# A graph layer with linear attention: mixed queries two chunks ahead, and VectorE reading PSUM in place of a second SBUF tensor

## The chip, the cores and the metric

The kernel runs on one core of a Trainium2 chip. The metric is the device time of one execution in microseconds (us). The engines are named as the profile names them: PE is TensorE's matmul pipe and PEld its weight load, DVE is VectorE, ACT is ScalarE, POOL is GpSimd, SP is SyncE, which here only issues DMAs. "Kernel before" and "changed kernel" are the two versions.

## The reference

N = 10000 nodes with D = 512 features, 160000 edges sorted by target node, everything in f32. One layer computes

```python
xn = layernorm(x)
# node sums (a graph convolution)
gnn = relu(segment_sum((xn @ W)[src] * edge_weight[:, None], dst) + bias)
# linear attention, 8 heads of 64
q, k, v = split(xn @ w_qkv.T)
q = softmax(q, over the 64 features of a head) * 64 ** -0.5
k = softmax(k, over the nodes)
mix = layernorm_gamma((q @ (k.T @ v)) @ w_out.T)          # context per head
x1 = x + gnn + mix
# experts: the mean over all nodes of layernorm(x1) chooses them, for all nodes alike
t = layernorm(x1)
p = softmax(mean(t, over nodes) @ router_w.T); two best -> weight of each of 6 experts
out = x1 + sum_e weight_e * (gelu(t @ W1[e] + b1[e]) @ W2[e] + b2[e])
```

## The kernel before, in words

**Chunks.** The nodes go in 20 chunks: 19 of 512 rows and one of 272. A chunk is a tile of 128 partitions (68 in the last) by 4 row blocks (`SUB`, index `s`) by 512 features.

**Stages**, with the places in the profiled execution's span where they lie:

1. 0 to about 195 us: rows of x are normalised (`normal_rows`) and written to `xn_d` in DRAM; the first three chunks of the next stage are already done here, and the tables of the edges are made.
2. to about 1285 us: for each chunk, keys `pk` and queries `pq` (L203 in `times`), exp of both on ACT, the softmax of the queries on DVE (`softmax_rows`, L182 to L188: a reduce over each head, a reciprocal, a multiply), the transposed queries `qT` written to DRAM, and the product `pc` (L780) of keys and normalised rows, summed into `G`.
3. to about 1355 us: `G`, the values' and the output's weights are folded into one 512 x 512 matrix `mix` (products `pctx`, `pmix`).
4. to about 2290 us, the attention stage: for each chunk, `attention` (L890 to L911) and the node sums (L929 to L946).
5. to the end, the feed-forward part (L1096 and around), which both versions have alike, but for the mean.

**Edges.** The 160000 edges are 1250 tiles of 128. `edges_in` gathers the source rows of each tile from `xn_d` by an indirect DMA that POOL issues (L483, tile `msg`, 24 buffers, up to 16 tiles ahead) and builds a selection matrix `sel` (six buffers) on DVE: for a whole group of 8 or 4 tiles at once, one comparison of a row of numbers with each edge's place in its window (L489), one multiplication by the edge's weight (L492), and a copy of one column (L495). `edges_summed` multiplies `sel` and `msg` on PE (`pm`, L504), ACT copies the result to `part` and stores it in `part_d` (L507, L508). There are 201 such groups. They are laid between the other matmuls of stages 2 and 4: after every product the code calls `work`, which adds the product's estimated PE time to a clock and then does as many groups as that time divided by `PACE` allows. So a smaller `PACE` puts more edge tiles into stage 2.

**Attention stage.** `attention(c)` loads the transposed queries `qT` (one buffer) and the rows of x again as `xt` (two buffers), multiplies by `mix` (`po`, L203), copies to `ot` on ACT (L903; three buffers), takes the row statistics (`row_stats`, bn_stats at L160, square root on ACT at L168), and on DVE normalises with gamma (L907) and adds `xt` (L909). It takes a function `beside`, which it calls ahead of its last row block. For the node sums of chunk c, `at` holds the rows gathered from `part_d` (`gathered`, L865, two buffers, an indirect DMA by POOL for each row block, after `far_enough` has put in the edge groups that those rows need). `nodes_rows` transposes `at` into `aT` (one buffer; PE's transposes `pt`, ACT's copies L197) and starts the gather of chunk c + 1. Then come four products with the graph weights (`pg`), the bias (L933, from PSUM into `et`, which is `at` itself), and one instruction over all four row blocks that takes the larger of `et` and 0 and adds `ot` (L934). The sum is stored as `x1_d` (L935), its row statistics are taken, it is normalised once more (L178) into `at`, or in the last chunk into the buffer `wg`, and the normalised rows are added up in `xsum` (L946) for the mean that chooses the experts.

In the kernel before, `attention(0)` precedes the loop, and iteration c calls `attention(c + 1)` with `nodes_rows` of chunk c as `beside`. So PE's order in an iteration is: three row blocks of `po` for chunk c + 1, the transposes for chunk c, the fourth `po`, four products `pg` for chunk c; edge groups stand between them.

**What sets the order.** PE's instructions run in the order in which the code lists them (`manual_schedule`). The other engines' orders are made by the planner of the tile framework from its own estimate of costs. SP's DMAs (`qT`, `xt`, the stores of `x1_d`) are one queue, ACT's (`qT_d`, `part_d`) another; POOL issues all gathers in one order.

**PSUM.** A pool of six banks serves `pk`, `pq`, `pc`, `po`, `pg` and the transposes in turn; two more serve `pm`. A bank is taken again when the engine that reads it is done.

**Mean.** After stage 4, `mean_row` sums `xsum` over partitions with a matmul against ones, adds the last chunk's normalised rows in the same way, and DVE multiplies by 1/N.

Of the kernel before, what the change touches and what calls it, by code (L numbers as in the profile page):

```python
# [9 lines left out]
F32 = mybir.dt.float32  # L10
I32 = mybir.dt.int32
AF = mybir.ActivationFunctionType
ALU = mybir.AluOpType
AX = mybir.AxisListType
# [3 lines left out]
P = 128  # L18
SQ = 32
SUB = 4  # L20
EPS = 1e-5
HEAD = 64
# [3 lines left out]
WIN = P // GROUP  # L26
# [1 line left out]
EARLY = 3  # L28
ROWS_SOON = 5
PRODUCT = 0.83  # L30
PACE = 0.93

AT_HAND = [(5, 320), (7, 384), (9, 448), (11, 512), (13, 576), (14, 640), (15, 672), (16, 704), (17, 736), (18, 756)]
CARRIES = [0, 128, 224, 320, 384, 448, 512, 576, 640, 672, 704, 736, 756]
# [12 lines left out]
def gps_layer_kernel(  # L47
# [19 lines left out]
    nc = tc.nc  # L67
    N, D = x.shape
# [18 lines left out]
    NCH = len(chunks)  # L87
# [5 lines left out]
    const = ctx.enter_context(tc.tile_pool(name="const", bufs=1))  # L93
# [34 lines left out]
    gamma_b = const.tile([P, D], F32, name="gamma_b")  # L128
    nc.scalar.dma_start(gamma_b, gamma.to_broadcast([P, D]))
    row_of = const.tile([P, NCH, SUB], I32, name="row_of")  # L130
    stats2 = const.tile([P, NCH, SUB, 2], F32, name="stats2")


# [42 lines left out]
    def normalize(o, t, r, mv, pool=0):  # L176
        for s in range(SUB):
            (nc.vector if s < SUB - pool else nc.gpsimd).tensor_scalar(  # L178
                o[:r, s, :], t[:r, s, :], mv[:r, s, 0:1], mv[:r, s, 1:2],
                op0=ALU.subtract, op1=ALU.mult)  # L180

    def softmax_rows(q, r, s):  # L182

        q3 = q[:r, s, :].rearrange("p (h e) -> p h e", e=HEAD)
        qs = small.tile([P, D // HEAD], F32, name="qs")
        nc.vector.tensor_reduce(qs[:r], q3, axis=AX.X, op=ALU.add)
        nc.vector.reciprocal(qs[:r], qs[:r])
        nc.vector.tensor_tensor(q3, q3, qs[:r, :, None].to_broadcast([r, D // HEAD, HEAD]), ALU.mult)  # L188

    def transposed(o, t, r, psum, tag, by_act=(1, 3)):  # L190

# [141 lines left out]
    with ExitStack() as ph:  # L333
# [139 lines left out]
        def edges_in(i):  # L473

            t0, batch = tiles_of(i)
            n = min(GROUP * batch, NET - t0)
            m = [None] * n
            for j in range(batch):
                for h in range(GROUP):
                    k = h * batch + j  # L480
                    if k < n:
                        m[k] = pools["m"].tile([P, D], F32, name="msg")
                        nc.gpsimd.indirect_dma_start(  # L483
                            out=m[k], out_offset=None, in_=xn_d,
                            in_offset=bass.IndirectOffsetOnAxis(ap=src_sb[:, t0 + k : t0 + k + 1], axis=0))
            sel = ew.tile([P, 2 * GROUP, WIN], F32, name="sel", bufs=6)
            if n < GROUP * batch:
                nc.vector.memset(sel[:, n:, :], 0.0)
            nc.vector.tensor_tensor(  # L489
                sel[:, :n, 1:], iota_w[:, None, :].to_broadcast([P, n, WIN - 1]),  # L490
                place[:, t0 : t0 + n, None].to_broadcast([P, n, WIN - 1]), ALU.is_equal)
            nc.vector.tensor_tensor(  # L492
                sel[:, :n, 1:], sel[:, :n, 1:],
                w_sb[:, t0 : t0 + n, None].to_broadcast([P, n, WIN - 1]), ALU.mult)
            nc.vector.tensor_copy(sel[:, :n, 0:1], on_w[:, t0 : t0 + n, None])  # L495
            return batch, m, sel

# [17 lines left out]
        held = {"edges": []}  # L515
# [229 lines left out]
        for c, (_, r) in enumerate(chunks):  # L745
# [23 lines left out]
            for s in range(SUB):  # L769
                pq = psum.tile([P, D], F32, name="pq", tag="ps")  # L770
                times(pq, xnT, s, r, wq)
                work(KB * PRODUCT)
                nc.scalar.activation(qt[:r, s, :], pq[:r], AF.Exp, scale=usable[:r])
                softmax_rows(qt, r, s)
            if c + 1 < NCH:
                xnT = turned_rows(c + 1, xn_next)
            for cb in range(KB):
# [63 lines left out]
        wg = wq  # L841
        nc.sync.dma_start(wg, gnn_w.rearrange("(k p) d -> p k d", p=P))
        nc.vector.memset(xsum, 0.0)
        io = query_ctx.enter_context(tc.tile_pool(name="c_io", bufs=2, side="right", reuse_waits="tile"))

        def far_enough(c):
# [28 lines left out]
            return qT  # L875

        def rows_again(c):
            xt = io.tile([P, SUB, D], F32, name="xt")
            nc.sync.dma_start(xt[: chunks[c][1]], tokens(x, c))
            return xt  # L880

# [6 lines left out]
        def attention(c, beside):  # L888


            r = chunks[c][1]
            qT = queries_in(c)
            xt = rows_again(c)
            ot = io.tile([P, SUB, D], F32, name="ot", bufs=3)
            for s in range(SUB):
                if s == SUB - 1:
                    beside()
                po = psum.tile([P, D], F32, name="po", tag="ps")
                times(po, qT, s, r, mix)
                put_out(KB * PRODUCT)  # L900
                if c == s == 0:
                    held["at"] = gathered(0)
                nc.scalar.copy(ot[:r, s, :], po[:r, :])  # L903
            mv = small.tile([P, SUB, 2], F32, name="mv")
            row_stats(ot, r, mv)
            for s in range(SUB):
                nc.vector.scalar_tensor_tensor(ot[:r, s, :], ot[:r, s, :], mv[:r, s, 0:1],  # L907
                                               gamma_b[:r], op0=ALU.subtract, op1=ALU.mult)
                nc.vector.scalar_tensor_tensor(ot[:r, s, :], ot[:r, s, :], mv[:r, s, 1:2],  # L909
                                               xt[:r, s, :], op0=ALU.mult, op1=ALU.add)  # L910
            return ot  # L911

        ot_next = attention(0, lambda: None)
        for c, (_, r) in enumerate(chunks):
            ot, at = ot_next, held["at"]
            aT = io.tile([P, KB, SUB * P], F32, name="aT", bufs=1)

            def nodes_rows():
# [1 line left out]
                if c + 1 < NCH:  # L920
                    held["at"] = gathered(c + 1)

            if c + 1 < NCH:
                ot_next = attention(c + 1, nodes_rows)
            else:
                nodes_rows()

            et = at
            for s in range(SUB):  # L929
                po = psum.tile([P, D], F32, name="pg", tag="ps")  # L930
                times(po, aT, s, r, wg)
                put_out(KB * PRODUCT)
                nc.vector.tensor_tensor(et[:r, s, :], po[:r, :], bias_b[:r], ALU.add)  # L933
            nc.vector.scalar_tensor_tensor(ot[:r], et[:r], 0.0, ot[:r], op0=ALU.max, op1=ALU.add)  # L934
            nc.sync.dma_start(x1_d[c], ot[:r])  # L935
            mv = stats2[:, c]
            row_stats(ot, r, mv)

            nt = et if c < NCH - 1 else wg
            normalize(nt, ot, r, mv)  # L940

            nc.vector.scalar_tensor_tensor(mv[:r, :, 0], mv[:r, :, 0], -1.0, mv[:r, :, 1],
                                           op0=ALU.mult, op1=ALU.mult)
            if c < NCH - 1:
                for s in range(SUB):
                    nc.vector.tensor_tensor(xsum[:r], xsum[:r], et[:r, s, :], ALU.add)  # L946
            if c == NCH - 3:
                sums_of_weights()
            if c == NCH - 2:
# [54 lines left out]
    def mean_row():  # L1004
        r = chunks[-1][1]
        nc.tensor.matmul(pmean, ones, xsum, start=True, stop=False)
        for s in range(SUB):
            nc.tensor.matmul(pmean, ones[:r], last[:r, s, :], start=False, stop=s == SUB - 1)
        mean_ctx.close()
        nc.vector.tensor_scalar(mean, pmean, 1.0 / N, None, op0=ALU.mult)  # L1010

    def mean_column():
        pr = psum_r.tile([P, D], F32, name="pr")
# [300 lines left out]
```

## Time and profile before

| | us |
|---|---|
| median of 10 executions | 3664.21 (3653.14 to 3674.59) |
| profiled execution | 3669.89 |
| its span | 3667.9, mean granted PE clock 0.958 |
| PE busy | 3370.1 (92%) |
| DVE busy | 1701.9 (46%) |
| POOL busy | 1470.4 (40%) |
| ACT busy | 794.9 (22%) |
| gathers of edges, L483 on POOL | 1250, 1257.0 in all, 1.006 each |
| `sel`, L489 and L492 on DVE | 201 each, 71.2 and 71.2 in all |
| L934 on DVE | 19 of 128 x 2048, 2.293 each |
| L178 on DVE in the attention stage | 76 of 128 x 512, 0.562 each |

The profile is of one execution. Busy times count an engine's own instructions, not its waits or its issuing of DMAs. The view in slices cuts the span into 40 equal parts and gives busy shares in tenths. In a list of waits, a line names the waiting engine, its tile and line, then what ended the wait. "issue" there means that the profile shows nothing that was waited for, "remote" that a signal came from another engine without its instruction being matched. In a line of the timeline the brackets hold the idle time of that engine just before the instruction. Idle time of an engine that is not the bound costs nothing by itself.

### The profile page before, as it was taken

To read this page: it belongs to the slowest core of one execution; us is meant where nothing else is said; L and a number is where in the kernel's file an instruction comes from. 1 tells how busy PE (TensorE), PEld (TensorE's weight loads), DVE (VectorE), ACT (ScalarE), POOL (GpSimd) and SP (SyncE) were. 2 spreads that over 40 slices of the span, in tenths; PEclk is the share of its full clock that TensorE was granted. 3 is DMA by queue.
4 is the path that set the end of the run, shared out by engine and by line. 5 is a ranking of instruction groups with operands and counts; after the bars stand their busy time and mean duration, and the time that the engine had idled before them with its cause. 6 is when DMAs were issued, how large, how long until landed. Compare 5 with 4: busy or idle time off the path is not lost. (4 is left out here: it accounts for less than half of the span.)

```text
span 3667.9 us, 36451 instructions
## 1 busy us (share of the span) xinstructions
PE 3370.1 (92%) x12967; PEld 1950.5 (53%) x12967; DVE 1701.9 (46%) x3899; ACT 794.9 (22%) x1626; POOL 1470.4 (40%) x1472
## 2 busy tenths in 40 slices
PE   6999998989999858988888999899999999999998
PEld 3433333333343323333333334788888888888877
DVE  7723333333343324545555557554454454454542
ACT  4411111111111111111121121322222222222221
POOL 7666666656666665767767652000000000000000
PEclk9999999999999978989999999999999999999999
DMA  9677777767777777878888875122212212221210
GB/s 360 253 230 213 246 224 230 235 207 233 229 225 224 212 237 235 269 255 297 285 277 290 277 253 150 45 76 58 69 58 58 81 47 58 81 55 49 81 36 36
DMA packets 218326, 644.91 MB, mean 176 GB/s; under 512 B 35486, under 2 KB 75422, under 8 KB 193786
## 3 DMA queue, kind: packets, MB, share of 16 engines
q0 software_dynamic: 108208, 354.02, 31.5%
q1 hardware_dynamic: 67656, 168.51, 14.4%
q10 hardware_dynamic: 42266, 119.91, 8.5%
q8 instruction: 106, 1.74, 0.2%
q14 instruction: 90, 0.74, 0.1%
HBM read 485.32 MB, written 157.00 MB: 175 GB/s over the span
## 5 line engine op out<-in xcount | busy, mean ns | idle before, releaser
L483 POOL DMA_INDIRECT msg<-xn_d,src_sb x1250 | 1257.0, 1006 | 661.6 <-issue 291.3
L504 PE MATMUL pm<-msg,sel 128*32 128x512 f32 x2504 | 380.1, 618 | 63.8 <-issue 51.0
L203 PE MATMUL pg<-wq,aT 128*128 128x512 f32 (+1 forms) x640 | 310.5, 633 | 41.6 <-issue 30.0
L780 PE MATMUL pc<-xn,ek 128*128 128x512 f32 (+1 forms) x640 | 307.4, 624 | 38.7 <-issue 22.1
L203 PE MATMUL po<-G,qT 128*128 128x512 f32 (+1 forms) x640 | 308.0, 626 | 18.1 <-issue 17.9
L203 PE MATMUL pq<-wq,xnT 128*128 128x512 f32 (+1 forms) x640 | 289.9, 601 | 7.5 <-issue 6.7
L203 PE MATMUL pk<-wk,xnT 128*128 128x512 f32 (+1 forms) x640 | 285.7, 597 | 0.6 <-issue 0.5
L507 ACT COPY part<-pm 128x512 f32<-128x512 f32 x201 | 117.8, 586 | 762.3 <-remote 365.0
L504 PEld LDWEIGHTS pm<-msg,sel 128*32 128x32 f32 x2504 | 72.6, 110 | 337.4 <-issue 304.4
L203 PEld LDWEIGHTS pg<-wq,aT 128*128 128x128 f32 (+1 forms) x640 | 120.7, 197 | 232.6 <-issue 200.9
L780 PEld LDWEIGHTS pc<-xn,ek 128*128 128x128 f32 (+1 forms) x640 | 122.8, 200 | 192.7 <-issue 168.1
L203 PEld LDWEIGHTS po<-G,qT 128*128 128x128 f32 (+1 forms) x640 | 121.0, 197 | 194.5 <-issue 184.4
L489 DVE TENSOR_TENSOR sel<-iota_w,place 128x248 f32<-128x248 f32 (+2 forms) x201 | 71.2, 354 | 325.1 <-remote 193.0
L1096 PE MATMUL px<-xnT,w_sb 128*128 128x256 f32 (+1 forms) x800 | 204.8, 379 | 11.1 <-DVE u L1131 11.0
L203 PEld LDWEIGHTS pq<-wq,xnT 128*128 128x128 f32 (+1 forms) x640 | 117.9, 188 | 178.4 <-issue 172.5
L203 PEld LDWEIGHTS pk<-wk,xnT 128*128 128x128 f32 (+1 forms) x640 | 117.7, 188 | 164.7 <-issue 158.4
L1096 PE MATMUL px<-w_sb,hh 128*128 128x256 f32 (+1 forms) x800 | 186.2, 380 | 0.0
L1096 PE MATMUL py<-xs,w_sum 128*128 128x256 f32 (+1 forms) x800 | 185.0, 374 | 0.0
L1096 PE MATMUL py<-w_sum,hh 128*128 128x256 f32 (+1 forms) x800 | 179.2, 379 | 0.0
L1096 PEld LDWEIGHTS px<-xnT,w_sb 128*128 128x128 f32 x800 | 150.7, 192 | 34.3 <-DVE u L1131 14.5
L160 DVE BATCH_NORM_STATS2 st<-ot 128x6 f32<-128x512 f32 (+1 forms) x160 | 106.7, 677 | 125.9 <-ACT ot L903 81.9
L1096 PEld LDWEIGHTS px<-w_sb,hh 128*128 128x128 f32 (+1 forms) x800 | 150.5, 188 | 22.9
(266 smaller groups left out, 4551.3 us busy)
## 6 DMA issues: line engine op xcount, KB each, us to landing
part_d<-part ACTq DMA_DIRECT2D x201, 256.0 KB
msg<-xn_d,src_sb POOLq DMA_INDIRECT x1250
xn<-in_x SPq DMA_DIRECT2D x19, 1024.0 KB
xn_d<-xn ACTq DMA_DIRECT2D x19, 1024.0 KB
qT_d<-qT ACTq DMA_DIRECT2D x19, 1024.0 KB
qT<-qT_d SPq DMA_DIRECT2D x19, 1024.0 KB
xt<-in_x SPq DMA_DIRECT2D x19, 1024.0 KB
x_d<-ot SPq DMA_DIRECT2D x19, 1024.0 KB
```

The lines of the kernel that those rows point to most:

```text
L160: nc.vector.bn_stats(st[:r, s, :], t[:r, s, :])
L203: nc.tensor.matmul(po[:r, :], t[:, kb, s * r : (s + 1) * r], w[:, kb, :], start=kb == 0, stop=kb == KB - 1)
L483: nc.gpsimd.indirect_dma_start(out=m[k], out_offset=None, in_=xn_d, in_offset=bass.IndirectOffsetOnAxis(ap=src_sb[:, t0 + k : t0 + k + 1], ...
L489: nc.vector.tensor_tensor(sel[:, :n, 1:], iota_w[:, None, :].to_broadcast([P, n, WIN - 1]), place[:, t0 : t0 + n, None].to_broadcast([P, n ...
L504: nc.tensor.matmul(pm[h * WIN : (h + 1) * WIN, :], sel[:, k, :], m[k] if k < len(m) else m[0], start=j == 0, stop=j == batch - 1, skip_gro ...
L507: nc.scalar.copy(part, pm)
L780: nc.tensor.matmul(pc, ek[:r, s, cb * P : (cb + 1) * P], xn[:r, s, :], start=s == 0, stop=s == SUB - 1)
L1096: nc.tensor.matmul(o, lhs[j], rhs[j], start=start and j == 0, stop=stop and j == n - 1, skip_group_check=True)
```

## The change

1. **Softmax of the queries.** ACT writes the exp back into the PSUM bank `pq` instead of into `qt`. DVE's reduce and multiply read the bank; the multiply writes `qt`.
2. **`sel`.** For each tile of a group one tensor_scalar compares and multiplies (two operands of one value a partition). There are 1250 of them in place of 402 instructions with broadcast operands.
3. **Order of the attention stage.** `attention(0)` and `attention(1)` precede the loop, and iteration c calls `attention(c + 2)`. The last two iterations have none. `ot` gets a fourth buffer, and `xt` keeps one.
4. **Node sums.** The bias is added inside the PSUM bank, and the maximum and the addition of `ot` follow row block by row block from PSUM. `at` is no longer written, so it is read by the transposes alone.
5. **Mean.** Only the last chunk is normalised. For the others, `xsum` collects each row times its reciprocal deviation, and `msum`, one value a partition, collects minus the mean times that reciprocal. `mean_row` sums `msum` by one more small matmul and adds the result as `shift`.
6. **`PACE`** goes from 0.93 to 0.945.

```diff
-PACE = 0.93
+PACE = 0.945
...
+    msum = const.tile([P, 1], F32, name="msum")
...
-    def softmax_rows(q, r, s):
+    def softmax_rows(q, r, s, e=None):
         q3 = q[:r, s, :].rearrange("p (h e) -> p h e", e=HEAD)
+        e3 = q3 if e is None else e[:r].rearrange("p (h e) -> p h e", e=HEAD)
         qs = small.tile([P, D // HEAD], F32, name="qs")
-        nc.vector.tensor_reduce(qs[:r], q3, axis=AX.X, op=ALU.add)
+        nc.vector.tensor_reduce(qs[:r], e3, axis=AX.X, op=ALU.add)
         nc.vector.reciprocal(qs[:r], qs[:r])
-        nc.vector.tensor_tensor(q3, q3, qs[:r, :, None].to_broadcast([r, D // HEAD, HEAD]), ALU.mult)
+        nc.vector.tensor_tensor(q3, e3, qs[:r, :, None].to_broadcast([r, D // HEAD, HEAD]), ALU.mult)
...
-            nc.vector.tensor_tensor(
-                sel[:, :n, 1:], iota_w[:, None, :].to_broadcast([P, n, WIN - 1]),
-                place[:, t0 : t0 + n, None].to_broadcast([P, n, WIN - 1]), ALU.is_equal)
-            nc.vector.tensor_tensor(
-                sel[:, :n, 1:], sel[:, :n, 1:],
-                w_sb[:, t0 : t0 + n, None].to_broadcast([P, n, WIN - 1]), ALU.mult)
+            for k in range(n):
+                nc.vector.tensor_scalar(sel[:, k, 1:], iota_w, place[:, t0 + k : t0 + k + 1],
+                                        w_sb[:, t0 + k : t0 + k + 1], op0=ALU.is_equal, op1=ALU.mult)
...
-                nc.scalar.activation(qt[:r, s, :], pq[:r], AF.Exp, scale=usable[:r])
-                softmax_rows(qt, r, s)
+                nc.scalar.activation(pq[:r], pq[:r], AF.Exp, scale=usable[:r])
+                softmax_rows(qt, r, s, pq)
...
+        nc.vector.memset(msum, 0.0)
...
-            xt = io.tile([P, SUB, D], F32, name="xt")
+            xt = io.tile([P, SUB, D], F32, name="xt", bufs=1)
...
-            ot = io.tile([P, SUB, D], F32, name="ot", bufs=3)
+            ot = io.tile([P, SUB, D], F32, name="ot", bufs=4)
...
-        ot_next = attention(0, lambda: None)
+        mixed = [attention(c, lambda: None) for c in range(2)]
         for c, (_, r) in enumerate(chunks):
-            ot, at = ot_next, held["at"]
+            ot, at = mixed.pop(0), held["at"]
...
-            if c + 1 < NCH:
-                ot_next = attention(c + 1, nodes_rows)
+            if c + 2 < NCH:
+                mixed.append(attention(c + 2, nodes_rows))
             else:
                 nodes_rows()
-            et = at
             for s in range(SUB):
                 po = psum.tile([P, D], F32, name="pg", tag="ps")
                 times(po, aT, s, r, wg)
                 put_out(KB * PRODUCT)
-                nc.vector.tensor_tensor(et[:r, s, :], po[:r, :], bias_b[:r], ALU.add)
-            nc.vector.scalar_tensor_tensor(ot[:r], et[:r], 0.0, ot[:r], op0=ALU.max, op1=ALU.add)
+                nc.vector.tensor_tensor(po[:r, :], po[:r, :], bias_b[:r], ALU.add)
+                nc.vector.scalar_tensor_tensor(ot[:r, s, :], po[:r, :], 0.0, ot[:r, s, :], op0=ALU.max, op1=ALU.add)
             nc.sync.dma_start(x1_d[c], ot[:r])
             mv = stats2[:, c]
             row_stats(ot, r, mv)
-            nt = et if c < NCH - 1 else wg
-            normalize(nt, ot, r, mv)
+            if c == NCH - 1:
+                normalize(wg, ot, r, mv)
             nc.vector.scalar_tensor_tensor(mv[:r, :, 0], mv[:r, :, 0], -1.0, mv[:r, :, 1],
                                            op0=ALU.mult, op1=ALU.mult)
             if c < NCH - 1:
                 for s in range(SUB):
-                    nc.vector.tensor_tensor(xsum[:r], xsum[:r], et[:r, s, :], ALU.add)
+                    nc.vector.scalar_tensor_tensor(xsum[:r], ot[:r, s, :], mv[:r, s, 1:2], xsum[:r],
+                                                   op0=ALU.mult, op1=ALU.add)
+                moved = small.tile([P, 1], F32, name="moved")
+                nc.vector.tensor_reduce(moved[:r], mv[:r, :, 0], axis=AX.X, op=ALU.add)
+                nc.vector.tensor_tensor(msum[:r], msum[:r], moved[:r], ALU.add)
...
-        nc.vector.tensor_scalar(mean, pmean, 1.0 / N, None, op0=ALU.mult)
+        pr = psum_r.tile([P, D], F32, name="pr")
+        nc.tensor.matmul(pr[0:1, 0:1], msum, ones, start=True, stop=True)
+        shift = wp.tile([1, 1], F32, name="shift")
+        nc.vector.tensor_copy(shift, pr[0:1, 0:1])
+        nc.vector.tensor_scalar(mean, pmean, shift, 1.0 / N, op0=ALU.add, op1=ALU.mult)
```

## The prediction

> **What bounds the kernel now.** I read the page from the top: engine shares, the 40 slices, then TensorE's (PE's) waits, then four stretches, then single instructions at the places the change touches. The profiled execution took 3669.89 us around a span of 3667.9; it stands 5.7 us (0.16%) above the median of ten, 3664.21. A difference under about 0.2% (7 us) can't be told from none here.
>
> Part 2 of the page, 40 slices of 91.7 us, digits in tenths:
>
> ```profile
> PE   6999998989999858988888999899999999999998
> PEclk9999999999999978989999999999999999999999
> POOL 7666666656666665767767652000000000000000
> ```
>
> PE is full nearly everywhere. Its thin places are slice 15 (mixing matrices) and slices 17 to 23 (attention and node sums), where the clock sags too. POOL, which issues the gathers, works only in the first 25 slices and is never full. By stretches (columns: PE, weight loads, DVE, ACT, POOL busy with counts, granted clock, DMA share, GB/s): keys and queries, start of the attention stage, its body, the FFN.
>
> ```profile
> 200.00:1285.00 1085.00, 1000.42 (x3569) 403.18 (x3572) 372.41 (x820) 180.56 (x294) 701.53 (x712) 0.96 0.73 225
> 1355.00:1415.00 60.00, 38.99 (x120) 15.10 (x119) 17.15 (x39) 9.52 (x17) 33.13 (x35) 0.80 0.68 212
> 1415.00:2181.00 766.00, 680.47 (x2198) 248.79 (x2200) 405.31 (x1077) 135.32 (x263) 524.60 (x502) 0.92 0.82 275
> 2290.00:3668.00 1378.00, 1349.72 (x6136) 1145.09 (x6134) 666.42 (x1355) 360.16 (x867) 0.00 (x0) 0.99 0.19 59
> ```
>
> PE idles 85 us in the keys and 86 in the attention body, 28 in the FFN. DVE is at 34% and 53% where the change works. So the order of PE's instructions, and waits in it, set the time. What it waited for (engine, operation, line, releaser: total us, times, longest):
>
> ```profile
> PE pm L504 <- issue: 51.0, 49, 5.1
> PE pg L203 <- issue: 30.0, 9, 7.2
> PE pg L203 <- ACT aT L197: 11.5, 3, 5.8
> PE pm L504 <- ACT part L507: 6.8, 3, 3.5
> PE pm L504 <- DMA msg<-xn_d,src_sb: 3.4, 4, 1.5
> ```
>
> A gathered message kept PE for 3.4 us in all; `sel`, built by DVE, never appears among the releasers. The big entries are "issue", which names no one.
>
> **Less contention (SBUF pairs replaced by PSUM).** Gathers (L483) that met no DVE instruction took 0.945 us; those that met only L188 (two SBUF inputs) 1.18; those under L186 or L933, which read one SBUF tensor or PSUM, 0.945. The extreme:
>
> ```profile
> 1683.42 2.29 DVE L934 SCALAR_TENSOR_TENSOR ot<-at,ot 128x2048 f32<-128x2048 f32 x1
> 1683.52 3.01 POOL L483 DMA_INDIRECT msg<-xn_d,src_sb  x1 [0.30 <-issue]
> ```
>
> What gathers took beyond 0.95 sums to 27 us in the keys and 46 in the attention stage; 20 of it under L934, 7 under L946, 4 each under L188 and L492. So the edit does relieve POOL. But each group's last message is issued 8 us or more (mostly 20) before its matmul and lands 2.3 us (median) after issue. What PE can gain is the 3.4 us of its message waits: **-3.4** (from 0 to -46, if the "issue" gaps are gathers in disguise). The Trainium skill's "SBUF — State Buffer", section Who interferes with whom, says that a DVE instruction with two SBUF inputs holds a port pair that GpSimd needs and that one with at most one does not; the rows agree. The same section says that tensor_scalar can take the pair in its two-port mode, which speaks against the new `sel`; ten gathers that met only L178, a tensor_scalar, took 1.015. By the rule's worst, 1,250 small locks would stretch gathers off PE's path; by the row the sum is unchanged.
>
> **`sel` by tile.** Gone are 201 L489 and 201 L492, 71.2 us each (142). New are 1,250 tensor_scalar of 31 elements. Nearest rows: L163, 4 elements, 217 ns; L178, 512 elements, 562 ns; a line between them gives 235 ns, so 294 us; at 0.16, L163's shortest kind, 200. DVE gains 58 to 152 us of work, 720 tiles of it in the keys (372 to at most 459 of 1085) and 530 in the attention stage. There normalising goes (76 x 562 = 38 us), L934 (43.6) becomes 76 x some 0.746 (57, from L909), L946 (51.6) likewise 57, two small ones per chunk add 8: about 457 of 766, 60%. The cover is depth: `sel` has six buffers and DVE waited 55.9 us for PE to give one back. Still, any late group delays PE; I take **+2**, between 0 and 152 (all of it on the path).
>
> **Softmax in PSUM.** The exp writes back into the bank, reduce and multiply read it, so the bank comes free after L188 instead of after L773. Durations don't change: L933 reads PSUM in 688 ns, L946 reads SBUF in 679. Banks go round six deep, so the sixth allocation after a query waits. With the traced times the multiply ended after the start of the matmul that takes its bank in eight chunks: 6.9 us in chunk 1, 1.8, 1.7, 1.2 (twice), 1.0, 0.5 and 0.4 in others, 14.7 in all. Chunk 1:
>
> ```profile
> 117.55 3.60 PE L780 MATMUL pc<-xn,ek 128*128 128x512 f32 x8
> 123.66 0.67 DVE L188 TENSOR_TENSOR qt<-qt,qs 128x512 f32<-128x512 f32 x1
> ```
>
> The matmul at 117.55 takes a bank that the changed kernel still holds at 124.33. DVE is full there (7 tenths), beside row statistics. The others are about a microsecond each, within the stage's idle time; I take chunk 1 alone, **+7**, between 0 (another DVE order) and 20 (each also late by a `sel`). The skill's "PSUM — Partial Sum Buffer", Summary: rules for kernel authors, says to evacuate promptly, which speaks against this edit; the sum by it would be the same sort of delay, unpriced.
>
> **Node sum in PSUM.** Two DVE steps now hold a bank instead of one, 0.75 us more. PE never waited on DVE in this stage, and the next bank user is six allocations off: 0, up to 0.75 x 80 = 60 if that cover goes. The chain after the last product gets shorter: 0.69 + 0.75 against 0.69 + 2.29, so row statistics start about 1.5 us sooner. ACT waited 33.0 us in 17 waits for `ve` before its square root (L168), and the copies of `part` and `aT` queue behind that. 17 x 1.55 = 26 us of ACT; PE's listed waits on those two copies come to 18.3. Most late copies show ACT itself waiting for PE's signal, so I take **-5**, between 0 and -18.
>
> **Two chunks ahead.** In the body each iteration has the same order on PE: three row blocks of attention, transposes, the fourth, four products. Its ends differ. `qT` has one buffer, so two attentions in a row wait for its load; today that happens once, after the change twice (0 to 1, 1 to 2):
>
> ```profile
> 1382.73 6.38 PE L203 MATMUL po<-G,qT 128*128 128x512 f32 x8 [7.95 <-issue]
> ```
>
> **+8** (plus up to 2.8: these eight took 6.38 us, the eight at 117.55 3.60). At the tail two chunks instead of one have no attention between transposes and products, and wait for `aT`:
>
> ```profile
> 2272.86 15.30 PE L203 MATMUL pg<-wq,aT 128*68 128x512 f32 x32 [5.79 <-ACT aT L197]
> ```
>
> **+5.8**, between 4 and 8. One `xt` buffer: the load (SP queue) waits for L909 of the chunk before; the qT load and `x1` stores stand on the same queue, but `xt` is read a whole iteration (45 us) later: 0, up to 8 once at the start. `at` now comes free with the transposes, so POOL loses 16.3 us of waits at L865 for `xsum`; PE waited for none of them: 0.
>
> **PACE and the mean.** 0.945 leaves about 16 of 720 edge tiles for the later stage. A key chunk costs 64.5 us with 42.3 tiles and 46 without: 0.44 a tile. An attention chunk costs 49 with 28.6 and 31.4 without: 0.615. So 16 x 0.175 = 2.8; the last groups are forced in at chunk borders either way, so **+1.5**, from -3 to 3. The mean gets a one-column matmul and a copy in a chain that PE already waits for (2.7 us at 2338, for `e_row`): **+1**, from 0 to 2.
>
> **Sum:** -3.4 + 2 + 7 - 5 + 8 + 5.8 + 1.5 + 1 = +16.9. From 3669.9 that is 3686.8; less the 5.7 by which the profiled execution lay above the median, 3681.
>
> **Rivals.**
> 1. *Faster: POOL was on the path.* The 30 + 51 us of "issue" before `pg` and `pm` appear while gathers run. If stretched gathers cause them, the attention stage's 46 us come back: -46 in place of -3.4 and the sum is -25.7, or 3638; with half of it, 3661, so more than 20 of the 46 must reach PE. For it: the clear stretch, and PE's idle lying in POOL's stages. Against: gathers issued 8 us ahead.
> 2. *No change:* PE's idle time swallows chunk 1's 7 us and ACT returns its full 18 instead of 5: 16.9 - 7 - 13 = -3.1, 3661, within the 7 us. For it: the idle of both stages. Against: chunk 1 lies where PE ran on without a pause.
> 3. *Slower still: DVE too late.* If a quarter of the 152 us of small instructions reaches PE in place of 2 (+36), 3717. For it: DVE at 60% with in-order row statistics ahead of `sel`. Against: six buffers and no wait on `sel` today.
>
> **How the numbers follow.** Forecast 0.38 (3671 to 3693, its own range), rival 1 0.36, rival 2 0.13, rival 3 0.13. So slower is 0.38 + 0.13 = 0.51, faster 0.36, same 0.13. The range goes from 3641, into rival 1, to 3706, into rival 3, leaving about a tenth at either end.
>
> **What would show it.** Right: a second wait of some 8 us before `po` after 1382, two waits of 5 to 6 on `aT` before 2290, a hole of 7 us near 117, gathers close to 0.95 us, and PE's idle in the body unchanged. Wrong: PE's "issue" gaps shrinking together with gather times (rival 1), or waits of PE on `sel`, or of `pq`/`po` banks on L188 or L934 (rival 3).

## The result, and the profile after

The changed kernel is slower: 3700.27 us (median of 18 runs, 3690.31 to 3712.5) against 3661.03 (62 runs of the kernel before, 3640.65 to 3683.6). The ratio is 1.0105, 95% interval 1.009 to 1.012, so 33 to 44 us. The forecast was slower by 17.

One thing has to be said ahead of all numbers. The runs fell on chips of two kinds (or on chips in two conditions; the traces don't say which), and the kernel before takes about 3400 us on the one and 3640 to 3660 on the other. The second and the third batch below, ten minutes apart, are both recorded under chip number 6, and they were of opposite kinds: if that number names one chip, the kind is a condition that comes and goes. "Kind of chip" below leaves this open. The runs of one batch share a chip number, so every ratio below is against the kernel before in the same batch. The traces tell the two kinds apart, and the change has opposite signs on them. The time above, the profile before and the profile after are all from the slower kind.

The page after, by slices:

```profile
PE   6898999988989947888889889899999999999998
POOL 7655666665666655666666662000000000000000
PEclk9999999999999978989989999899999999999999
```

Counted from one, PE lost a digit in the 2nd and 4th slice (the 2nd holds chunks 1 and 2 of the keys), the 10th, 12th, the 15th to 17th (mixing matrices and around), the 23rd and 24th, gained one in the 7th, 14th and 22nd, and is as before in the last 16. The same stretches as before (PE, weight loads, DVE, ACT, POOL busy with counts, granted clock, DMA share, GB/s):

```profile
200.00:1285.00 1085.00, 994.12 (x3550) 404.60 (x3550) 455.02 (x1352) 177.48 (x291) 675.60 (x695) 0.96 0.71 222
1355.00:1415.00 60.00, 32.27 (x86) 12.78 (x87) 17.88 (x53) 7.34 (x12) 30.04 (x32) 0.72 0.58 184
1415.00:2181.00 766.00, 659.94 (x2195) 245.51 (x2194) 432.99 (x1299) 132.71 (x261) 492.30 (x501) 0.92 0.81 272
```

DVE went from 372 to 455 us in the keys, POOL from 525 to 492 in the attention body. Both were foreseen. What PE waited for, some lines of the list of waits:

```profile
PE pm L503 <- issue: 43.0, 29, 7.7
PE po L205 <- DMA qT<-qT_d: 23.4, 2, 14.6
PE pc L779 <- DVE qt L190: 17.2, 5, 11.4
PE pg L205 <- ACT aT L199: 16.0, 5, 7.6
PE pt L197 <- DVE qt L190: 4.1, 2, 3.1
PE pt L197 <- DMA at<-part_d,row_of: 3.7, 2, 3.5
```

The multiply of the softmax (L190) now stops PE, for 21.3 us in all; before the same line stopped it for 0.7. The bank is held. But 11.4 of the 21.3 are one wait, at 758, where the exp itself came late (ACT's wait for it is "remote", 9.3 us), and the kernel before has such waits of `pc` on the exp too, 6.6 us in two. Chunks 1 and 2 make 8.2. The load of `qT` stops PE twice. "Issue" before `pm` and `pg` fell from 51.0 and 30.0 us to 43.0 and 8.2. The groups on POOL and DVE:

```profile
L485 POOL DMA_INDIRECT msg<-xn_d,src_sb x1250 | 1219.9, 976 | 720.4 <-issue 298.8
L492 DVE TENSOR_SCALAR sel<-iota_w,place,w_sb 128x31 f32<-128x31 f32 x1250 | 303.6, 314 | 347.6 <-remote 251.7
```

The gathers became shorter (1.006 to 0.976 us), and `sel` takes 304 us of DVE instead of 142.

Where the time went by stage, from the starts of matmuls in the two traces (us after the first matmul):

| | before | after | difference |
|---|---|---|---|
| keys of chunk 3 | 161.6 | 183.3 | +21.7 |
| end of the last keys' product `pk` | 1219.5 | 1230.7 | +11.2 |
| first `po` | 1329.2 | 1355.7 | +26.5 |
| first `px` (FFN) | 2267.8 | 2306.6 | +38.8 |
| last `px` | 3635.7 | 3673.9 | +38.2 |

Much of it is lost before chunk 3, though less than the first row says. Ahead of chunk 3 stand the small products `pnext`, and up to them PE is 12.9 us late. PE's timeline before, then after:

```profile
181.12 0.61 PE L549 MATMUL pnext<-ident,bases 1*128 1x1 f32 x13
193.97 0.56 PE L548 MATMUL pnext<-ident,bases 1*128 1x1 f32 x11
```

The rest of the 21.7 is mostly unnamed gaps among these small products, some 8 us; in the kernel before such gaps begin only behind the start of chunk 3, at 196.6. At the keys of chunk 4 the difference is 14.9 (238.8 against 223.9), at the end of the keys 11.2. There 744 edge tiles instead of 760 lie ahead of the first `po` (at the 0.44 us a tile of the prediction, 7 us). The mixing stage loses 15, and the attention stage, which carries those 16 tiles, 12 (16 tiles at the prediction's 0.615 are 9.8).

### The profile page after: what moved, and what is told of

Read it like the earlier page. It is cut to its first block, busy times and chain, and to the rows that moved or that the text cites. A ratio compares the mean times of both kernels' runs of the same rounds, so it can differ in the third digit from the quotient of the medians.

```text
span 3706.3 us, 37367 instructions
## 1 busy us (share of the span) xinstructions
PE 3367.0 (91%) x12969; PEld 1953.1 (53%) x12969; DVE 1835.8 (50%) x4771; ACT 791.2 (21%) x1626; POOL 1428.3 (39%) x1472
## 4 chain that ended last, share of the span: by engine, by line
PE 53%; DMA 4%; another core or an unknown queue 3%; issue 3%; DVE 2%; ACT 0%; ACTq 0%; POOL 0%; DVEq 0%; SPq 0%
PE px L1103 13%; PE pz L1103 9%; PE py L1103 9%; PE po L205 8%; PE pg L205 7%; PE pm L503 4%; PE ph L1103 2%; DMA z_d<-xt 1%; PE pt L197 1%; DMA xt<-x_d 1%; DMA part_d<-part 0%; DMA at<-part_d,row_of 0%; DMA qT<-qT_d 0%; DVE xt L1200 0%
## 5 line engine op out<-in xcount | busy, mean ns | idle before, releaser
L485 POOL DMA_INDIRECT msg<-xn_d,src_sb x1250 | 1219.9, 976 | 720.4 <-issue 298.8
L492 DVE TENSOR_SCALAR sel<-iota_w,place,w_sb 128x31 f32<-128x31 f32 x1250 | 303.6, 314 | 347.6 <-remote 251.7
L503 PE MATMUL pm<-msg,sel 128*32 128x512 f32 x2504 | 359.2, 623 | 59.2 <-issue 43.0
L205 PE MATMUL po<-G,qT 128*128 128x512 f32 (+1 forms) x640 | 320.5, 643 | 50.4 <-issue 25.0
```

What stands on the lines that cost most here:

```text
L205: nc.tensor.matmul(po[:r, :], t[:, kb, s * r : (s + 1) * r], w[:, kb, :], start=kb == 0, stop=kb == KB - 1)
L485: nc.gpsimd.indirect_dma_start(out=m[k], out_offset=None, in_=xn_d, in_offset=bass.IndirectOffsetOnAxis(ap=src_sb[:, t0 + k : t0 + k + 1], ...
L492: nc.vector.tensor_scalar(sel[:, k, 1:], iota_w, place[:, t0 + k : t0 + k + 1], w_sb[:, t0 + k : t0 + k + 1], op0=ALU.is_equal, op1=ALU.mult)
L503: nc.tensor.matmul(pm[h * WIN : (h + 1) * WIN, :], sel[:, k, :], m[k] if k < len(m) else m[0], start=j == 0, stop=j == batch - 1, skip_gro ...
```

## The experiments

All times are medians of five rounds beside the kernel before. The parts are named as in the list of the change.

**Single parts, first batch.** The kernel before took 3401.09 us here. The softmax alone:

```diff
...
-                nc.scalar.activation(qt[:r, s, :], pq[:r], AF.Exp, scale=usable[:r])
-                softmax_rows(qt, r, s)
+                nc.scalar.activation(pq[:r], pq[:r], AF.Exp, scale=usable[:r])
+                softmax_rows(qt, r, s, pq)
```

> The kernel before with the softmax of the queries in PSUM alone. The whole change costs 39 us, and its products already start 21.7 us late at chunk 3, where PE waits for the multiply that frees a query's bank. Bank theory: this part alone costs 10 to 20 us, and most of it shows before the keys of chunk 4 (its start 10 or more later than in the kernel before). DVE-crowding theory: without the small sel instructions the multiplies come in time, and it costs 0 to 5. Contention theory: gathers under the multiply (1.18 us in the kernel before) fall to 0.95, and it gains up to 5.

3403.96 us, ratio 1.0012 (1.0002 to 1.0022): 3 us slower, in the range of the DVE-crowding theory. The keys of chunk 3 start at 163.4.

`sel` alone:

```diff
-            nc.vector.tensor_tensor(
-                sel[:, :n, 1:], iota_w[:, None, :].to_broadcast([P, n, WIN - 1]),
...
+            for k in range(n):
+                nc.vector.tensor_scalar(sel[:, k, 1:], iota_w, place[:, t0 + k : t0 + k + 1],
+                                        w_sb[:, t0 + k : t0 + k + 1], op0=ALU.is_equal, op1=ALU.mult)
```

> The kernel before with one tensor_scalar per edge tile for sel alone. Bank theory: the 160 us that DVE gets more (1250 at 314 ns against 402 at 354) lie in its idle time, -3 to +5. DVE-crowding theory: PE waits longer for what DVE does beside sel (sums of G, copies of xnT, multiplies), +10 to +20. No wait of PE on sel in either.

3395.99 us, ratio 0.999 (0.9981 to 1.0): 5 us faster in medians, 0 to 6 by the interval, the lower end of the bank theory's -3 to +5. Chunk 3 starts at 160.6. PE never waits for `sel`.

Two chunks ahead alone (PACE 0.93):

```diff
-            xt = io.tile([P, SUB, D], F32, name="xt")
+            xt = io.tile([P, SUB, D], F32, name="xt", bufs=1)
...
-            ot = io.tile([P, SUB, D], F32, name="ot", bufs=3)
+            ot = io.tile([P, SUB, D], F32, name="ot", bufs=4)
...
-        ot_next = attention(0, lambda: None)
+        mixed = [attention(c, lambda: None) for c in range(2)]
...
-            if c + 1 < NCH:
-                ot_next = attention(c + 1, nodes_rows)
+            if c + 2 < NCH:
+                mixed.append(attention(c + 2, nodes_rows))
```

> The kernel before with the attention two chunks ahead alone (one xt buffer, four ot buffers). End-cost theory: two waits for qT at the start of the attention stage (8.8 and 14.6 in the changed kernel against 8.0 once) and one more chunk at the tail without attention beside it, +15 to +25 in all. Rival: the body of the stage gains what the ends lose, because ot is there a chunk earlier, -5 to +5.

3406.18 us, ratio 1.0021 (1.0011 to 1.003): 5 us slower, below the expected 15 to 25 and at the upper end of the rival's -5 to +5.

Node sums in PSUM and the mean:

```diff
...
-                nc.vector.tensor_tensor(et[:r, s, :], po[:r, :], bias_b[:r], ALU.add)
-            nc.vector.scalar_tensor_tensor(ot[:r], et[:r], 0.0, ot[:r], op0=ALU.max, op1=ALU.add)
+                nc.vector.tensor_tensor(po[:r, :], po[:r, :], bias_b[:r], ALU.add)
+                nc.vector.scalar_tensor_tensor(ot[:r, s, :], po[:r, :], 0.0, ot[:r, s, :], op0=ALU.max, op1=ALU.add)
...
-            nt = et if c < NCH - 1 else wg
-            normalize(nt, ot, r, mv)
+            if c == NCH - 1:
+                normalize(wg, ot, r, mv)
...
-                    nc.vector.tensor_tensor(xsum[:r], xsum[:r], et[:r, s, :], ALU.add)
+                    nc.vector.scalar_tensor_tensor(xsum[:r], ot[:r, s, :], mv[:r, s, 1:2], xsum[:r],
+                                                   op0=ALU.mult, op1=ALU.add)
...
```

> The kernel before with the node sums in PSUM and the mean without normalised rows. Contention theory: the gathers no longer stretch under the 2.29 us instruction, and DVE has 24 us less, so it gains 5 to 30. Off-path theory: messages were there early anyway, gain 0 to 5. Bank rival: the node sums' banks are held 0.75 us longer and PE waits, +5 to +20. It must pay 1 us for the added matmul in the mean.

3374.09 us, ratio 0.9934 (0.9918 to 0.995). By itself this part gains 27 us.

By medians these add to -24, not +39. The page of the run with the softmax alone says why this chip is another kind:

```profile
PE   6999999999999889999999989999999999999998
PEclk9999999999999899999999999999999999999999
```

Its list of PE's waits begins:

```profile
PE pm L505 <- DMA msg<-xn_d,src_sb: 30.0, 29, 3.2
PE pn L524 <- ACT sq L521: 22.2, 2, 20.2
PE po L204 <- DMA qT<-qT_d: 10.1, 1, 10.1
```

There is no "issue" line. PE is 97% busy, and what it waits for most are gathered messages: 30 us in 29 waits, 26 of the 30 in the attention stage, where the kernel before on the other kind waited 3.4 in all. The messages are later here against PE: in the attention stage the last gather of a group is issued 6.6 us (median) before the group's first product, against 26 in the kernel before on the other kind. The unnamed gaps are gone, and behind them the gathers are what PE waits for.

**The whole change beside its parts, second batch.** The kernel before took 3400.17 us.

The edit is none: it is the changed kernel as it stands.

> The changed kernel once more, beside single parts on one chip. On the chip of the single parts the kernel before took 3401 us, 260 less than where the change was first measured, and the parts gave +4 (softmax), -5 (sel), +5 (two ahead) and -27 (node sums and mean), in medians. If parts add up and this chip is such a one: -20 to -25 plus 1 to 3 for PACE. If the parts hurt each other (bank held, DVE 50% busy): +5 to +40. On a chip where PE has unnamed gaps and the kernel before takes 3660: +30 to +45 as measured.

3382.46 us, ratio 0.9952 (0.9937 to 0.9966): the same code that lost 39 us gains 18 here. Adding up, with the 1 to 3 for PACE, was -17 to -24; the interval, -21 to -12, does not rule it out.

The changed kernel with the softmax in SBUF:

```diff
...
-                nc.scalar.activation(pq[:r], pq[:r], AF.Exp, scale=usable[:r])
-                softmax_rows(qt, r, s, pq)
+                nc.scalar.activation(qt[:r, s, :], pq[:r], AF.Exp, scale=usable[:r])
+                softmax_rows(qt, r, s)
```

> The changed kernel with the softmax of the queries back in SBUF. Bank theory: on a chip with unnamed gaps this takes back 15 to 25 of the 39 us (chunk 3 then starts as in the kernel before); on one without gaps only 2 to 6, as the part alone cost 4.

3375.11 us, ratio 0.9926 (0.9912 to 0.994), 7 less than the whole change; alone the softmax cost 3. The timelines of PE show where. The whole change on this chip:

```profile
124.31 8.73 PE L779 MATMUL pc<-xn,ek 128*128 128x512 f32 x16 [3.01 <-DVE qt L190]
171.62 0.63 PE L197 MATMUL pt<-ident,xn 128*128 128x128 f32 x4 [1.63 <-DVE qt L190]
192.75 14.00 PE L205 MATMUL pk<-wk,xnT 128*128 128x512 f32 x32
```

With the softmax in SBUF:

```profile
174.46 1.64 PE L196 MATMUL pt<-ident,qt 128*128 128x128 f32 x13 [1.48 <-DVE qt L189]
183.56 14.00 PE L204 MATMUL pk<-wk,xnT 128*128 128x512 f32 x32
```

The last line of each is the start of the keys of chunk 3: 192.75 against 183.56. In the first, PE's products and transposes of rows wait for the multiply, since they take banks that queries still hold. Measured from the first matmul, chunk 3 starts at 159.6 with the node sums alone, at 160.6 with `sel` alone, at 163.4 with the softmax alone, at 163.3 in the whole change without the softmax, and at 172.6 in the whole change. Of the 13.0 us from 159.6 to 172.6, the softmax alone makes 3.8 and the change without it 3.7; the other 5.5 come only when the two meet. The 9.3 us between the whole change and the one without the softmax are still there at the end of the keys (1077.1 against 1067.8). A few us of these are not firm: the run below, one chunk ahead, has the same code up to there and starts chunk 3 at 176.2.

The changed kernel one chunk ahead (PACE stays at 0.945):

```diff
-            xt = io.tile([P, SUB, D], F32, name="xt", bufs=1)
+            xt = io.tile([P, SUB, D], F32, name="xt")
...
-            ot = io.tile([P, SUB, D], F32, name="ot", bufs=4)
+            ot = io.tile([P, SUB, D], F32, name="ot", bufs=3)
...
-        mixed = [attention(c, lambda: None) for c in range(2)]
+        ot_next = attention(0, lambda: None)
...
-            if c + 2 < NCH:
-                mixed.append(attention(c + 2, nodes_rows))
+            if c + 1 < NCH:
+                ot_next = attention(c + 1, nodes_rows)
```

> The changed kernel with the attention one chunk ahead again (two xt, three ot buffers). End-cost theory: 13 to 25 us less than the changed kernel on a chip with gaps (it waited 23.4 us for qT there), 5 to 10 less on one without, where the part alone cost 5. Rival, that two chunks ahead is what the other parts need for their gain: no less, or more.

3392.92 us, ratio 0.9978 (0.9969 to 0.9987), 10 slower than the whole change: the rival's side. It seemed that the ahead order is what the other parts need.

The node sums and mean alone (same edit as above), once more:

> The node sums in PSUM and the mean without normalised rows alone, once more. Contention theory, as where PE waited 30 us for messages: 20 to 30 us faster than the kernel before. On a chip with unnamed gaps, where messages kept PE 3.4 us, it should gain only 0 to 10.

3373.8 us, ratio 0.9921 (0.9906 to 0.9936). The gain stands. What carries it, summed over the 485 edge gathers of the attention stage on this kind of chip: the time beyond 0.95 us was 47, 42 and 44 us in the three runs with L934 as it was (softmax, `sel`, ahead alone), 19 and 23 in the two with the node sums in PSUM. Their attention stage, from the first `po` to the first `px`, took 850, 848 and 853 us against 822 and 830. So some 23 us less of stretched gathers go with some 24 us less of attention stage. PE's listed waits for messages there fell by less, from 26 to 28 us to 18 and 23; its edge products, from the start of one matmul to the next, took 187 to 200 us against 175 and 179. That the shorter gathers do this, and not the shorter work of DVE or the earlier release of `at` in the same part, is argued and not shown. The group of gathers with the softmax alone, then with the node sums alone (first batch):

```profile
L484 POOL DMA_INDIRECT msg<-xn_d,src_sb x1250 | 1256.7, 1005 | 412.1 <-issue 230.2 <-DMA msg<-xn_d,src_sb 74.3 <-PE pm L505 43.8
```

```profile
L484 POOL DMA_INDIRECT msg<-xn_d,src_sb x1250 | 1234.7, 988 | 411.4 <-issue 218.5 <-DMA msg<-xn_d,src_sb 85.1 <-PE pm L505 46.3
```

**Halves of the change, third batch.** The kernel before took 3641.81 us: this is the kind with gaps. Two chunks ahead with node sums and mean, PACE 0.93 (the two edits above together):

```diff
...
-        ot_next = attention(0, lambda: None)
+        mixed = [attention(c, lambda: None) for c in range(2)]
...
+                nc.vector.tensor_tensor(po[:r, :], po[:r, :], bias_b[:r], ALU.add)
+                nc.vector.scalar_tensor_tensor(ot[:r, s, :], po[:r, :], 0.0, ot[:r, s, :], op0=ALU.max, op1=ALU.add)
```

> The kernel before with two chunks ahead and the node sums and mean of the changed kernel, softmax and sel as before, PACE 0.93. If two chunks ahead help once the gathers are free (the changed kernel was 10 us faster than without it): 30 to 37 us faster than the kernel before on a chip without unnamed gaps. If parts just add (-27 and +5): 20 to 24. On a chip with gaps, if softmax and sel make the loss there: -10 to +10; if the ends of the attention stage do: +15 to +30.

3642.46 us, ratio 0.9994 (0.9972 to 1.0015): no change that can be told.

Softmax in PSUM with `sel` by tile (the added lines alone):

```diff
...
+                nc.scalar.activation(pq[:r], pq[:r], AF.Exp, scale=usable[:r])
+                softmax_rows(qt, r, s, pq)
...
+            for k in range(n):
+                nc.vector.tensor_scalar(sel[:, k, 1:], iota_w, place[:, t0 + k : t0 + k + 1],
+                                        w_sb[:, t0 + k : t0 + k + 1], op0=ALU.is_equal, op1=ALU.mult)
```

> The kernel before with the softmax in PSUM and sel by tile together. Alone they made 3 and -5 us, and the keys of chunk 3 started at 163.4 and 160.6 (from the first product), against 172.6 in the whole change. If they hurt each other, because DVE is full beside the first chunks and the bank waits for the multiply: chunk 3 at 170 to 176, and 8 to 15 slower in all. If the two just add: chunk 3 at 164, -3 to +3. On a chip with gaps the first: +15 to +25.

3669.39 us, ratio 1.0078 (1.0049 to 1.0106), so 18 to 39 us slower, 28 in medians. This pair carries most of the loss of the change. The keys of chunk 3 start at 179.6 after the first matmul, 18.0 later than in the other run of this batch (161.6); the whole change stood at 183.3. PE's timeline (its own span):

```profile
125.97 9.70 PE L778 MATMUL pc<-xn,ek 128*128 128x512 f32 x16 [2.75 <-DVE qt L189]
175.08 0.63 PE L196 MATMUL pt<-ident,xn 128*128 128x128 f32 x4 [2.45 <-DVE qt L189]
199.82 1.01 PE L204 MATMUL pk<-wk,xnT 128*128 128x512 f32 x1 [1.94 <-issue]
201.93 1.01 PE L204 MATMUL pk<-wk,xnT 128*128 128x512 f32 x1 [1.10 <-issue]
```

The same waits as on the other kind, and then the unnamed gaps, between single matmuls of 1.01 us. PE's waits for the multiply come to 13.0 us in this run. Where the rest of the 28 is lost this trace doesn't show: it is of the fastest of six executions (3655.99), against the other run of the batch it is 18.0 us late at chunk 3, 6.0 at the end of the keys and 9.8 at the first `px`.

**Fourth batch.** The kernel before took 3401.22 us, a chip without gaps again. `sel` alone, same edit:

> The sel part alone once more. On a chip with unnamed gaps, where softmax and sel together cost 28 us: bank theory (the held bank needs both parts, a late DVE and a bank that waits for it): -5 to +8, and chunk 3 starts within 3 us of the kernel before; DVE-crowding theory (the small instructions alone): +15 to +30. On a chip without gaps -6 to 0 as before.

3394.35 us, ratio 0.998 (0.9969 to 0.9992). On this kind of chip the part gains a little, as before. The split on the other kind, which part of the pair does what there, was not seen.

Two chunks ahead with node sums and mean, same edit:

> Two chunks ahead with node sums and mean, once more. On a chip without unnamed gaps the sums alone gained 26 and 27 us, and two chunks ahead gave 10 within the whole change and cost 5 alone. If the ahead order pays once the gathers are free: 30 to 37 us faster than the kernel before; if the parts add: 20 to 24. On a chip with gaps no change again, -10 to +5.

3385.75 us, ratio 0.9955 (0.9941 to 0.9968): a gain of 15, less than either expectation, and 11 less than the sums alone. So the ahead order costs 5 alone and 11 beside the sums when PACE is 0.93. That takes back the reading of the run one chunk ahead. There and in the whole change PACE was 0.945, with 506 edge tiles in the attention stage instead of 490, and that stage took 845 us one chunk ahead against 825 two chunks ahead. Whether the ahead order pays only with the larger PACE, or `sel` has to do with it, was not tried.

No version was seen to beat the kernel before on both kinds of chip. The node sums and mean alone are the fastest seen on the kind without gaps (0.9934 and 0.9921); on the other they were run only together with the ahead order, which gave no change.

## Why the prediction was right or wrong

**Sign and bound.** Slower was forecast, and the time lies in the stated range. The sign held for the kind of chip that the prediction's profile came from, and the result fell on that kind: this was luck, since on the other kind the same code is 18 us faster. The size was not right: +39 against +16.9, outside the forecast's own 3671 to 3693 and about halfway from 3681 to rival 3's 3717. The step that failed is the pair of terms "Softmax in PSUM, +7" and "`sel` by tile, +2", mis-sized at 9 where the two together measured 28 (18 to 39). The other terms, without PACE, summed to +6.4 with the ahead order and the sums; measured -2 (-10 to +5). What is left, about 12, lies in PACE and in the halves acting on each other, and the intervals of the two halves are nearly as wide as that. In the traces a like amount lies in the mixing stage: from the end of the last `pk` to the first `po` it takes 125.0 us in the changed kernel, against 109.7 before and 107.9 and 109.5 in the two halves. What lengthens it there stays open.

**Softmax.** The mechanism was right: the bank that waits for the multiply, first beside the row statistics of the first chunks. The prediction priced it with the multiply's place in the old trace and took the new `sel` as hidden in DVE's idle time. But the stage that mattered was the one where DVE had little (7 to 8 tenths; in chunk 2 it works without a pause from 150.5 to 178), and there `sel` is 42 small instructions and 6 copies, 10.4 us, in place of 9 and 5, 4.0 us, and DVE takes them ahead of the softmax. The first reduce of chunk 2 in the kernel before, then the end of `sel`, the first reduce and PE's wait in the changed kernel:

```profile
161.14 0.68 DVE L186 TENSOR_REDUCE qs<-qt 128x8 f32<-128x512 f32 x1
169.01 1.38 DVE L492 TENSOR_SCALAR sel<-iota_w,place,w_sb 128x31 f32<-128x31 f32 x6
170.38 0.68 DVE L188 TENSOR_REDUCE qs<-pq 128x8 f32<-128x512 f32 x1
172.27 0.63 PE L197 MATMUL pt<-ident,xn 128*128 128x128 f32 x4 [3.14 <-DVE qt L190]
```

The four multiplies of chunk 2 end at 172.1 to 177.9 instead of 162.8 to 168.5. On the chip without gaps the softmax alone makes chunk 3 3.8 us late and the whole change 13.0, as above. The 20 us kept as the term's upper end, "each also late by a `sel`", named this case but was not chosen, and it is still less than the 28 of the pair. On the kind with gaps neither part was run alone, so that `sel` by itself makes part of the loss there is not ruled out.

**`sel`.** The count came out near its upper end: 304 us of DVE against 294. Alone it costs nothing where it could be measured. Six buffers hid it from PE's matmuls, as argued; they did not hide it from DVE's other customers.

**Less contention.** Here the prediction was wrong in a way that the result hides. It took 3.4 us as all that PE could gain. Where PE has no unnamed gaps, the part that relieves POOL is worth 27 us, more than half of rival 1's 46 and probably through the gathers, but not as the rival told it: it shortens edge products, and there are no "issue" gaps to shorten. Where PE has gaps, messages are early (26 us ahead of their products, above) and the relief has little to give: stretching of the attention stage's gathers fell from 45 to 16 us in the changed kernel, and 45 to 22 with the ahead order and the sums, without a gain that can be told. So the 3.4 was a true reading of a trace from one chip, not of the kernel. The rule in the Trainium skill's "SBUF — State Buffer", section Who interferes with whom, agrees with the runs on the two SBUF inputs: gathers that met only the multiply took 1.18 us when it read SBUF (L188) and 0.944 in the changed kernel, where it reads PSUM (L190, 12 gathers). Its warning about tensor_scalar did not show for `sel`: in the changed kernel 83 gathers that met only L492 took 0.945 us, like those that met nothing. For L178, of 512 elements, the 1.015 of the prediction stands on its side.

**Node sum in PSUM.** The -5 was to come from ACT, waiting less for `ve`. It didn't: 57.3 us in 21 waits before, 58.8 in 18 after, over the whole run. The cover of the banks held: PE's list has no wait for a bank of the node sums.

**Two chunks ahead.** The second wait for `qT` came, larger than the 8 foreseen: 23.4 us in two waits in place of 7.95 in one. Both waits of the changed kernel, in PE's timeline:

```profile
1402.29 5.86 PE L205 MATMUL po<-G,qT 128*128 128x512 f32 x8 [8.77 <-DMA qT<-qT_d]
1437.18 3.77 PE L205 MATMUL po<-G,qT 128*128 128x512 f32 x4 [14.62 <-DMA qT<-qT_d]
```

The 5.8 at the tail, a second wait of `pg` for `aT`, did not come so. The transposes of the last chunk waited for their gather instead, 3.7 us in the list above, 9.3 with the part alone.

**Forecast signs.** Of the five signs of being right, the hole near 117 came (twice over, in chunks 1 and 2), the second `qT` wait came, and gathers came close to 0.95 (0.976 on average). The body's idle, told as unchanged, rose from 86 to 106 us of 766. The tail's two waits on `aT` did not come as told. Of the signs of being wrong two came as well: the "issue" gaps before `pm` and `pg` shrank together with the gathers' times (81 to 51 us), which was rival 1's sign, and yet the kernel was slower; and PE waited on the multiply for banks, 9.9 us without the one wait at 758, which was rival 3's.

**Slips of reading.** Four readings of the prediction are off, and none moves its sum. The clock's digits sag in slices 15, 16 and 18, not 17 to 23. POOL's waits at L865 for `xsum` are three, 27.0 us, not 16.3. 76 x 562 ns is 42.7 us; the 38 is the row's busy time. The two lines of chunk 1 are 6.8 us apart, not 6.9.

**PACE and the mean** were not run by themselves. Nothing shows the +1.5 and +1 right or wrong.

## What to carry to other kernels

A resource that is held longer is to be priced in the stage where the engine that releases it has no room, with the other edits' work already put there; two edits that each cost little can meet on one engine. An idle time that the profile gives to nobody may belong to the chip or its condition and not to the kernel: if it fills the path, it hides the next limit, and what a change is worth there says little of its worth without it. So a change is compared with its predecessor on the same chip and at the same time, and a sign that turns between chips is told with both.

## What the runs showed of the hardware that was not expected

The same kernel took 3400 to 3401 us in three batches and 3642 to 3661 in the others. The feed-forward stage hardly differs: 1368 us from first to last `px` in the kernel before and 1365 in the run with the softmax alone on the faster kind. Nearly all of the difference lies in the stages with gathers: 1329 against 1154 us to the first `po`, and 939 against 850 in the attention stage. On the slower kind PE has gaps of one to a few us between matmuls that wait for nothing named, many waits of ACT and DVE end with a signal that the profile matches to nothing ("remote"), and the granted clock of the profiled executions is 0.951 to 0.962 against 0.983 to 0.989. The lateness can be measured at the copies of `part`. Where ACT had been idle, the copy began 0.14 us (median) after the last edge product in all ten traces of the faster kind. In the four of the slower kind it began 1.1 to 1.5 us after it, and in a tenth of the cases over 6. ACT's waits between 300 and 1000 us in the span, first the kernel before on the slower kind, then the node sums alone on the faster (second batch):

```profile
ACT part L507 <- remote: 111.5, 15, 19.4
ACT qt L773 <- remote: 49.4, 9, 9.3
```

```profile
ACT part L508 <- PE pm L505: 196.0, 66, 8.2
ACT qt L774 <- PE pq L204: 136.9, 49, 2.9
```

In the first the profile finds no instruction that ended when ACT was let go; in the second it is mostly the matmul. What makes signals late there, and whether the gathers have to do with it, stays open: no run was made to find it.

The small tensor_scalar also cost more than the line through L163 and L178 had it: 314 ns for 31 elements, against 235.
